# Turns of the second layer's x between the products, two kinds of stores on another queue, and a shared first normalization

## The chip, the cores and the metric

The kernel runs on one core of a Trainium2 chip. The metric is the time of one execution on the device in microseconds; of several runs the median is given. A profiled execution is a run of its own, and the trace is taken from it.

## The reference

Two layers of the same kind are applied to x of shape (32, 32, 64, 256): 32 samples s, 32 places b, 64 channels, 256 positions l. Each layer normalizes x over 32 groups of 8 positions, convolves it along l with weights that are different for every b and l, and adds the result to x. The weights and the bias come from two small networks on z.

```python
h = relu(layernorm(z @ W1 + b1, g1, be1))            # (b, l, 128)
w = (h @ W2 + b2).reshape(B, L, CI, CO, K)           # weights of their own for every b and l
hb = relu(layernorm(z @ Wb1 + bb1, gb1, beb1))
bias = (hb @ Wb2 + bb2).transpose(0, 2, 1)
xp = pad(x, one zero at either end of l)
x_uf = stack([xp[..., i:i + L] for i in range(3)], axis=-1)
conv = einsum('sbilk,bliok->sbol', x_uf, w) + bias[None]
x = x + conv(groupnorm(x))                           # layer 0, then layer 1 with its own parameters
```

In the document the first and the second layer are called layer 1 and layer 2.

## The kernel before

All is in float32. A unit is four places b and a quarter of l (64 positions); a layer has 32 units, so u runs from 0 to 63, and each unit is done in two halves of the output channels. The steps are numbered v = 2u + h, from 0 to 127. `weights(v, k)` for k from 0 to 11 makes one piece of the convolution's weights on TensorE (`make`, lines 633 and 634, into a PSUM tile `pg`, of which there are three) and moves it with the bias b2 into `wall` (`take`, VectorE in line 645, ScalarE in line 656 for half of the third kind). `products(v)` multiplies the normalized x (`xn`) with `wall` in four quarters (line 687, into PSUM tiles `pc`, of which there are two), and VectorE adds each quarter to the residual in `ring` (line 696).

The order of all instructions on each engine is the order of the program text, written out by hand. Step v runs the twelve pieces of `weights(v)`; `products(v - 1)` stands behind the matmuls of the first piece and ahead of its `take`. Behind piece k stand the functions that `agenda(v)` has put into `todo[k]`: statistics, stores, loads (all on the queue of SP), normalization (`normalize`, line 619, on GpSimd) and the addition of the bias to the residual two steps ahead (`add_bias`, line 577, on GpSimd).

The normalized x of a unit stands with samples and places across the free axis in `xn`, which has room for two units. In layer 1 x is loaded in that order from the host's array. In layer 2 x is what layer 1 has stored (`x1`): `parts_of_half` (line 172) loads half of a unit's places with four DMAs into `raw` (first halves) or `land` (second halves), and `turn_half` (line 190) turns it on VectorE in two transpositions of 33 blocks of 32 x 32, one for each pair of places, behind pieces 2 and 3 of a step. `next_half` then normalizes it in place.

Before step 1 stands `first_phase`. Its twenty rounds i compute the hidden layers of both networks in eight batches (`Batch`; tiles of staging lie in `xn` and `raw`, which have no x yet), store the hidden activations (hd, line 317) and the bias (bd, line 339) in DRAM, take statistics of the first groups (line 464), and make the weights of step 0 from round 7 on. At its end `Merge` and `Table` lay out mean and deviation (`tab`), and `starting` normalizes unit 0 in four cuts on VectorE; the cuts 2 and 3 stand between the quarters of `products(0)`.

Of the kernel before, what the change touches and what calls it, by code (L numbers as in the profile page):

```python
# [43 lines left out]
def conv_layers(  # L44
# [142 lines left out]
    def turn_half(u, k, t, buf):  # L187

        src = at(buf[:, t * CH * MT : t * CH * MT + 1], [[1, MH], [MT, CH]])
        nc.vector.transpose(xn[:, u % 2, k * NT // 2 + t], src)  # L190
# [36 lines left out]

    class Batch:


        def __init__(self, nets, zt, zp, zs, j):
            self.j, self.zt, self.zp, self.zs = j, zt, zp, zs
            self.w = nets[j * NR // (UL // 2)]
            flat = xn.rearrange("p n t j s -> p (n t j s)")
            o = 0

            def take(n):
                nonlocal o
                o += n
                return flat[:, o - n : o]  # L240

            ht = [take(2 * BLK) for _ in range(2)]
            self.bs = [take(BLK // 2).rearrange("p (t a m) -> p t a m", t=NT, a=2) for _ in range(4)]
            self.var = take(2 * NR * NR)
            o = flat.shape[1] // 2
            self.ht = [[take(2 * BLK) for _ in range(2)], ht]
            self.q = take(BLK)
            self.zq = take(2 * BLK).rearrange("p (n f) -> p n f", n=2)

# [37 lines left out]
        def turn(self):  # L287
            p = ps_g.tile([P, 2, BLK], FP, tag="pg", name="pz")
            for net in range(2):
                for b in range(NR):  # L290
                    nc.tensor.transpose(
                        p[:, net, b * P : (b + 1) * P],
                        self.zs[:, net, b * NR : (b + 1) * NR].rearrange("p r a -> p (r a)"),
                        ident,
                    )
            nc.scalar.copy(self.zq, p)

        def hidden(self, net):
# [8 lines left out]
            for k in range(2):  # L307
# [7 lines left out]
                if net:  # L315
                    continue
                nc.sync.dma_start(out=hd[self.j * NR // 2 + k], in_=self.ht[0][k])

        def bias(self, i):
            n = 2 * M  # L320
            p = ps_c.tile([P, n], FP, tag="pc", name="pb")
            for b in range(2):
# [16 lines left out]
            nc.sync.dma_start(  # L339
                out=bd[i].rearrange("t b o l -> (b o) t l"), in_=bs.rearrange("p t a m -> p t (a m)")  # L340
# [105 lines left out]
    def first_phase(first_weights, first_bias, add_bias, starting):  # L446
# [22 lines left out]
        with tc.tile_pool(name="stage", bufs=1) as stage:  # L469
# [36 lines left out]
            for i in range(needed + 2):  # L506
# [20 lines left out]
                if i == needed + 1:  # L527
                    merge.mean()
                    merge.root()
                    table.expand(nc.vector)  # L530
                stats(i, range(2))
# [21 lines left out]
                if i == needed + 1:  # L553
                    table.lay(table.spread(), [nc.vector.tensor_copy, nc.scalar.copy])
                    starting(0)
                    starting(1)
# [5 lines left out]
    with tc.manual_schedule():  # L562
# [113 lines left out]
        def products(v, between=None):  # L676
            u, h = divmod(v, NH)
            n = u // UL
            y = residual(v)
            eb = EB // 2  # L680
            for q in range(NB):
                pc = ps_c.tile([P, EB, CH], FP, tag="pc", name="pc")
                for p in range(q * eb, (q + 1) * eb + 1):
                    n0, n1 = max(2 * p - 2, q * EB), min(2 * p + 2, (q + 1) * EB)
                    a = p * F + (n0 - 2 * p) * CH
                    for t in range(NT):
# [7 lines left out]
                        )  # L694
                part = y[:, :, :, q * eb : (q + 1) * eb]
                nc.vector.tensor_tensor(part, pc.rearrange("p (m a) o -> p a o m", a=2), part, ALU.add)  # L696
                if between:
                    between(q)
# [70 lines left out]
        def starting():  # L769
# [5 lines left out]
            def cut(q):  # L775
                if q < NB:
                    for k in range(2):
                        normalize(0, k, bufs[k], nc.vector, cuts[q], cuts[q + 1])
# [19 lines left out]
        def agenda(v):  # L798
# [9 lines left out]
            if UL <= half[0] < U:  # L808
                for t in range(NT // 2):
                    todo[2 + t].append(lambda t=t: turn_half(*half, t, place_half(*half)))  # L810
            todo[3 if half[0] >= UL else 2].append(lambda: next_half(*half))
# [8 lines left out]
            elif x < U:  # L820
                for i, part in zip((1, 1, 4, 4), parts_of_half(x, k, place_half(x, k))):
# [141 lines left out]
```

## Time and profile before

| | us |
|---|---|
| median of 3 runs | 3988.72 |
| lowest and highest run | 3983.26, 3991.18 |
| the profiled execution | 3984.39 |
| its span in the trace | 3982.6 |

The page of the profile gives for each engine the time in which it was busy, as a share of the span. PE is TensorE's matmuls, PEld its loading of weights, which overlaps them; DVE is VectorE, ACT ScalarE, POOL GpSimd, SP the engine that issues the DMAs. L645 is line 645 of the kernel. A row of the waits gives who waited for whom, the sum in microseconds, how often, and the longest. A row of the timeline gives start, duration, engine, line, operation, the tiles as out<-in, the shapes, and in brackets the idle time of the engine ahead of it with what ended it; xN at the end joins N such instructions in a row.

### The profile page before, as it was taken

The page shows a single profiled execution, that of the slowest core. Times are in us where ns is not written, and L with a number is a line of the kernel's source. Part 1 is how long each engine was busy: PE and PEld are TensorE (multiplying, and loading weights), DVE is VectorE, ACT ScalarE, POOL GpSimd, SP SyncE. Part 2 cuts the span into 40 slices and gives each one's busy share as a digit, 9 for nine tenths or more (in the row PEclk, how much of TensorE's full clock was granted, in tenths as well). Part 3 has the DMA queues.
Part 4 walks back from the last instruction along what each step waited for, and adds up shares of the span by engine and source line. Part 5 has one row for each costly group of instructions (what it writes and reads, how often), then busy time and mean ns, then how long its engine had stood idle before and what let it go on. Part 6 is the DMA issues. An engine that isn't in the chain of part 4 may idle for free.

```text
span 3982.6 us, 185486 instructions
## 1 busy us (share of the span) xinstructions
PE 3792.1 (95%) x86548; PEld 3663.0 (92%) x86548; DVE 2813.2 (71%) x3086; ACT 1278.0 (32%) x4399; POOL 1864.3 (47%) x655
## 2 busy tenths in 40 slices
PE   6799999999999999999999999999999999999999
PEld 3699999999999999999989999999999999999998
DVE  5777777777777776767676766666666667666765
ACT  3332333323333333333332332232233223322232
POOL 2255455454554545445444455455445444544452
PEclk8899999999999999999999999999999999999999
DMA  8765655656555554545565555565555555555552
GB/s 288 266 204 173 208 167 196 189 176 207 165 197 189 192 161 135 174 134 172 162 174 143 156 138 133 154 154 134 137 152 150 133 142 155 142 132 146 155 136 87
DMA packets 136756, 657.76 MB, mean 165 GB/s; under 512 B 38312, under 2 KB 45872, under 8 KB 70192
## 3 DMA queue, kind: packets, MB, share of 16 engines
q1 hardware_dynamic: 135984, 645.89, 55.2%
q8 instruction: 677, 11.09, 1.2%
q14 instruction: 95, 0.78, 0.1%
HBM read 496.91 MB, written 148.90 MB: 162 GB/s over the span
## 4 chain that ended last, share of the span: by engine, by line
PE 81%; DVE 8%; issue 7%; DMA 2%; ACT 0%; DVEq 0%; POOL 0%; SPq 0%; ACTq 0%; POOLq 0%
PE pg L633 51%; PE pc L687 24%; PE pg L634 5%; DVE wall L645 5%; DVE xn L190 3%; DMA out_dram<-ring 1%; DMA hd<-xn 0%; ACT xn L308 0%; DMA land<-in_xg_dram 0%; PE spread L422 0%; PE ph L306 0%; DVE ring L696 0%; PE over L377 0%; PE pb L324 0%; DMA hT<-hd 0%
## 5 line engine op out<-in xcount | busy, mean ns | idle before, releaser
L633 PE MATMUL pg<-hT,w2t 128*64 128x128 f32 x24576 | 2754.7, 274 | 118.7 <-DVE wall L645 100.1
L633 PEld LDWEIGHTS pg<-hT,w2t 128*64 128x64 f32 x24576 | 2686.6, 137 | 166.0 <-DVE wall L645 115.8
L634 PE MATMUL pg<-hT,w2t 128*64 128x128 f32 x24576 | 2754.7, 274 | 3.2 <-issue 2.9
L634 PEld LDWEIGHTS pg<-hT,w2t 128*64 128x64 f32 x24576 | 2687.1, 137 | 2.5 <-issue 2.3
L645 DVE TENSOR_TENSOR wall<-pg,b 128x1024 f32<-128x1024 f32 (+1 forms) x1540 | 1866.9, 1218 | 525.7 <-PE pg L634 520.3
L656 ACT ACTIVATE wall<-pg,b 64x128 f32<-64x128 f32 x4064 | 1152.6, 468 | 2586.6 <-DVE wall L645 2586.5
L687 PE MATMUL pc<-wall,xn 128*32 128x128 f32 (+1 forms) x36864 | 946.8, 262 | 24.8 <-issue 18.9
L687 PEld LDWEIGHTS pc<-wall,xn 128*32 128x32 f32 x36864 | 909.8, 110 | 63.3 <-issue 58.0
L577 POOL TENSOR_TENSOR ring<-ring,bt 128x2048 f32<-128x2048 f32 x127 | 580.4, 4570 | 772.0 <-DMA bt<-bd 431.4
L619 POOL TENSOR_TENSOR xn<-xn,tab 128x2112 f32<-128x2112 f32 x190 | 891.1, 4690 | 15.0
L696 DVE TENSOR_TENSOR ring<-pc,ring 128x512 f32<-128x512 f32 x512 | 354.1, 692 | 582.5 <-PE pc L687 504.4
L613 POOL COPY xn<-edge 64x64 f32<-64x64 f32 x96 | 22.3, 232 | 930.9 <-DVE xn L190 589.8
L619 POOL TENSOR_TENSOR xn<-raw,tab 128x2112 f32<-128x2112 f32 x54 | 254.0, 4703 | 172.0 <-PE pc L687 124.1
L347 DVE BATCH_NORM_STATS2 parts<-ring 128x6 f32<-128x256 f32 x512 | 192.2, 417 | 6.5
L190 DVE STREAM_TRANSPOSE xn<-land 128x1056 f32<-128x1056 f32 x64 | 132.6, 2071 | 0.0
L190 DVE STREAM_TRANSPOSE xn<-raw 128x1056 f32<-128x1056 f32 x64 | 132.2, 2066 | 0.0
L739 DVE BATCH_NORM_STATS2 first_parts<-land 128x6 f32<-128x512 f32 x168 | 114.2, 680 | 5.5 <-DMA land<-in_xg_dram 5.4
L439 POOL COPY tab<-spot 64x1024 f32<-64x1024 f32 x28 | 29.0, 1036 | 72.1 <-ACT spot L426 71.2
L282 POOL TENSOR_TENSOR raw<-w2t,xn 128x256 f32<-128x256 f32 x16 | 10.1, 629 | 107.4 <-DVE xn L277 107.4
L464 DVE BATCH_NORM_STATS2 first_parts<-ring 128x6 f32<-128x512 f32 x72 | 44.6, 679 | 10.5 <-DMA ring<-in_xg_dram 10.4
L306 PE MATMUL ph<-xn,wc 17*128 17x512 f32 x128 | 34.6, 745 | 16.4 <-ACT xn L308 6.5
L306 PEld LDWEIGHTS ph<-xn,wc 17*128 17x128 f32 x128 | 9.9, 206 | 35.0 <-ACT xn L308 13.5
(88 smaller groups left out, 413.0 us busy)
## 6 DMA issues: line engine op xcount, KB each, us to landing
bt<-bd SPq DMA_DIRECT2D x508, 256.0 KB, 11.9
ring<-in_xs_dram SPq DMA_DIRECT2D x64, 1024.0 KB, 9.5
x<-ring SPq DMA_DIRECT2D x64, 1024.0 KB, 5.0
ring<-x SPq DMA_DIRECT2D x64, 1024.0 KB, 10.2
out_dram<-ring SPq DMA_DIRECT2D x64, 1024.0 KB, 5.1
raw<-in_xp_dram SPq DMA_DIRECT2D x55, 1056.0 KB, 12.3
land<-in_xg_dram SPq DMA_DIRECT2D x46, 1024.0 KB, 8.4
raw<-x SPq DMA_DIRECT2D x128, 256.0 KB, 8.6
```

What stands on the lines that cost most here:

```text
L190: nc.vector.transpose(xn[:, u % 2, k * NT // 2 + t], src)
L347: nc.vector.bn_stats(out, y[:, :, :, g * e : (g + 1) * e])
L464: nc.vector.bn_stats(first_parts[:, g, bg], slots[order[i]][:, k])
L577: nc.gpsimd.tensor_tensor(y, y, bts.pop(v).rearrange("p o (a m) -> p o a m", a=2), ALU.add)
L619: eng.tensor_tensor(o, i, tab[:, x, None, j0:j1].to_broadcast(list(o.shape)), op)
L633: nc.tensor.matmul(pg[0:C, k, :], w[:, k0 * C : (k0 + 1) * C], h0, start=True, stop=True)
L634: nc.tensor.matmul(pg[C:P, k, :], w[:, k1 * C : (k1 + 1) * C], h1, start=True, stop=True)
L645: nc.vector.tensor_tensor(place(rows, a), pg[rows].rearrange("p o (t m) -> p t m o", t=NT), b2[n][rows, kind, None, None, o0 : o0 + OG].to ...
L656: nc.scalar.activation(place(rows, a)[:, :, :, k], pg[rows, k].rearrange("p (t m) -> p t m", t=NT), AF.Identity, bias=b2[n][rows, kind, o0 ...
L687: nc.tensor.matmul(pc[t * S : (t + 1) * S, n0 - q * EB : n1 - q * EB, :], xn[:, u % 2, t, p, :], wall[:, t, a : a + (n1 - n0) * CH], start ...
L696: nc.vector.tensor_tensor(part, pc.rearrange("p (m a) o -> p a o m", a=2), part, ALU.add)
L739: nc.vector.bn_stats(first_parts[:, g, bg], lands[i % LAND])
```

## The change

- In layer 2 each transposition of a half is cut in two (17 and 16 columns), and the four instructions of a half are put into `products(u, h)` for the half h of the next unit: two ahead of the eviction of the first quarter, one behind that, one behind the second. `next_half` for that half stands behind piece 0 of the next step, and the loads of a half (`parts_of_half`) stand one step later than before.
- The stores of hd and bd are issued from ScalarE's queue. Each is owed until the next call of `pay`, which stands behind a later instruction of ScalarE.
- `q` of a batch lies in `raw`, and `bs`, the bias on its way to bd, lies in the second half of `xn`, no more in the first.
- The laying out of the first table and the first two cuts of `starting` stand ahead of the last round's statistics; of each cut the first pair of places is normalized on VectorE and the second on GpSimd.

```diff
-    def turn_half(u, k, t, buf):
-        src = at(buf[:, t * CH * MT : t * CH * MT + 1], [[1, MH], [MT, CH]])
-        nc.vector.transpose(xn[:, u % 2, k * NT // 2 + t], src)
+    def turns_of_half(u, k, buf):
+        def turn(t, j0, j1):
+            i = t * CH * MT + j0
+            src = at(buf[:, i : i + 1], [[1, j1 - j0], [MT, CH]])
+            nc.vector.transpose(xn[:, u % 2, k * NT // 2 + t, j0:j1], src)
+        cuts = (0, MH // 2 + 1, MH)
+        return [lambda t=t, c=c: turn(t, *c) for t in range(NT // 2) for c in zip(cuts, cuts[1:])]
...
+    owed = []
+    def pay(*stores):
+        for f in owed:
+            f()
+        owed[:] = stores
...
+            self.q = raw[:, 2 * BLK : 3 * BLK]
...
-            self.bs = [take(BLK // 2).rearrange("p (t a m) -> p t a m", t=NT, a=2) for _ in range(4)]
             self.var = take(2 * NR * NR)
...
-            self.q = take(BLK)
             self.zq = take(2 * BLK).rearrange("p (n f) -> p n f", n=2)
+            self.bs = [take(BLK // 2).rearrange("p (t a m) -> p t a m", t=NT, a=2) for _ in range(4)]
...
             nc.scalar.copy(self.zq, p)
+            pay()
...
                 if net:
-                    continue
-                nc.sync.dma_start(out=hd[self.j * NR // 2 + k], in_=self.ht[0][k])
+                    pay()
+                else:
+                    pay(lambda k=k: nc.scalar.dma_start(out=hd[self.j * NR // 2 + k], in_=self.ht[0][k]))
...
-            nc.sync.dma_start(
-                out=bd[i].rearrange("t b o l -> (b o) t l"), in_=bs.rearrange("p t a m -> p t (a m)")
+            pay(
+                lambda: nc.scalar.dma_start(
+                    out=bd[i].rearrange("t b o l -> (b o) t l"), in_=bs.rearrange("p t a m -> p t (a m)")
+                )
             )
...
+                if i == needed + 1:
+                    table.lay(table.spread(), [nc.vector.tensor_copy, nc.scalar.copy])
+                    starting(0)
+                    starting(1)
+                    pay()
                 stats(i, range(2))
...
-                if i == needed + 1:
-                    table.lay(table.spread(), [nc.vector.tensor_copy, nc.scalar.copy])
-                    starting(0)
-                    starting(1)
...
+            turns = turns_of_half(u + 1, h, place_half(u + 1, h)) if UL <= u + 1 < U else []
...
+                if turns and q == 0:
+                    turns.pop(0)()
+                    turns.pop(0)()
                 part = y[:, :, :, q * eb : (q + 1) * eb]
                 nc.vector.tensor_tensor(part, pc.rearrange("p (m a) o -> p a o m", a=2), part, ALU.add)
+                if turns:
+                    turns.pop(0)()
...
-                    for k in range(2):
-                        normalize(0, k, bufs[k], nc.vector, cuts[q], cuts[q + 1])
+                    for k, eng in enumerate((nc.vector, nc.gpsimd)):
+                        normalize(0, k, bufs[k], eng, cuts[q], cuts[q + 1])
...
-            if UL <= half[0] < U:
-                for t in range(NT // 2):
-                    todo[2 + t].append(lambda t=t: turn_half(*half, t, place_half(*half)))
-            todo[3 if half[0] >= UL else 2].append(lambda: next_half(*half))
+            if half[0] < UL:
+                todo[2].append(lambda: next_half(*half))
+            if u + 1 >= UL:
+                todo[0].insert(0, lambda: next_half(u + 1, h))
...
-            elif x < U:
-                for i, part in zip((1, 1, 4, 4), parts_of_half(x, k, place_half(x, k))):
+            if UL <= half[0] < U:
+                for i, part in zip((1, 1, 4, 4), parts_of_half(*half, place_half(*half))):
```

## Rows read from the trace of the kernel before

**Rows 1.** The page: span, and each engine's busy time, share and instructions.
```profile
span 3982.6 us, 185486 instructions
...
PE 3792.1 (95%) x86548; PEld 3663.0 (92%) x86548; DVE 2813.2 (71%) x3086; ACT 1278.0 (32%) x4399; POOL 1864.3 (47%) x655
```
**Rows 2.** Waits of TensorE's weight loads in 1000:2000 (layer 1): us, times, longest.
```profile
PEld pg L633 <- DVE wall L645: 1.8, 1, 1.8
```
**Rows 3.** The same in 2100:3900 (layer 2).
```profile
PEld pg L633 <- DVE wall L645: 102.9, 59, 1.8
```
**Rows 4.** Timeline of VectorE, one step of layer 2.
```profile
2479.01 1.22 DVE L645 TENSOR_TENSOR wall<-pg,b 128x1024 f32<-128x1024 f32 x1 [0.52 <-PE pg L634]
2482.72 0.69 DVE L696 TENSOR_TENSOR ring<-pc,ring 128x512 f32<-128x512 f32 x1 [2.49 <-PE pc L687]
2484.41 0.69 DVE L696 TENSOR_TENSOR ring<-pc,ring 128x512 f32<-128x512 f32 x1 [1.00 <-PE pc L687]
...
2492.68 2.07 DVE L190 STREAM_TRANSPOSE xn<-land 128x1056 f32<-128x1056 f32 x1
...
2495.70 2.07 DVE L190 STREAM_TRANSPOSE xn<-land 128x1056 f32<-128x1056 f32 x1
...
2512.69 0.69 DVE L696 TENSOR_TENSOR ring<-pc,ring 128x512 f32<-128x512 f32 x1 [2.49 <-PE pc L687]
```
**Rows 5.** Timeline of VectorE, first evictions of two steps at the end.
```profile
3914.70 0.69 DVE L696 TENSOR_TENSOR ring<-pc,ring 128x512 f32<-128x512 f32 x1 [2.49 <-PE pc L687]
...
3942.96 0.69 DVE L696 TENSOR_TENSOR ring<-pc,ring 128x512 f32<-128x512 f32 x1 [2.49 <-PE pc L687]
```
**Rows 6.** Lines 190 and 390 on VectorE: count, ns minimum/median/maximum, first and last.
```profile
L190 DVE STREAM_TRANSPOSE xn<-raw x64: 1999/2070/2107, 1972.1 to 3867.7; 128x1056 f32<-128x1056 f32 x64
...
L390 DVE TENSOR_TENSOR apart<-over,moments x9: 144/157/163, 153.0 to 2047.6; 128x8 f32<-128x8 f32 x5, 128x9 f32<-128x9 f32 x1, 128x2 f32<-128x2 f32 x1, 128x6 f32<-128x6 f32 x1
```
**Rows 7.** Timelines of VectorE and GpSimd, a turn beside the laying of a table.
```profile
2462.68 2.03 DVE L190 STREAM_TRANSPOSE xn<-raw 128x1056 f32<-128x1056 f32 x1
...
2462.44 1.03 POOL L439 COPY tab<-spot 64x1024 f32<-64x1024 f32 x1 [9.96 <-ACT spot L426]
```
**Rows 8.** Loads into `raw`: SP's timeline, and time to landing in 2100:3900.
```profile
2493.25 1.16 SPq L172 DMA_DIRECT2D raw<-x  x2
...
DMA to landing us min/median/max: 5.4/8.6/12.8
```
**Rows 9.** Timeline of GpSimd in the step of rows 4.
```profile
2498.44 9.46 POOL L619 TENSOR_TENSOR xn<-xn,tab 128x2112 f32<-128x2112 f32 x2
2507.90 4.57 POOL L577 TENSOR_TENSOR ring<-ring,bt 128x2048 f32<-128x2048 f32 x1
```
**Rows 10.** The first products: timelines of TensorE and VectorE, and the chain of work.
```profile
165.70 0.45 PE L633 MATMUL pg<-hT,w2t 128*64 128x128 f32 x1 [8.35 <-issue]
...
169.38 2.52 PE pc L687 x72
...
166.54 0.76 DVE L619 TENSOR_TENSOR xn<-land,tab 128x576 f32<-128x576 f32 x1 [3.82 <-DMA bd<-xn]
...
182.36 0.69 DVE L696 TENSOR_TENSOR ring<-pc,ring 128x512 f32<-128x512 f32 x1 [0.66 <-PE pc L687]
```
**Rows 11.** Timeline of VectorE, first statistics of a piece in step 1.
```profile
200.66 0.69 DVE L739 BATCH_NORM_STATS2 first_parts<-land 128x6 f32<-128x512 f32 x1 [5.43 <-DMA land<-in_xg_dram]
```
**Rows 12.** First phase: ScalarE, TensorE, line 339, and busy time by engine in 60:70.
```profile
51.14 4.63 ACT L308 ACTIVATE xn<-ph,vec 128x1024 f32<-128x1024 f32 x4 [3.31 <-DMA hd<-xn]
...
68.98 0.45 PE L633 MATMUL pg<-hT,w2t 128*64 128x128 f32 x1 [5.01 <-DMA hT<-hd]
...
L339 SPq DMA_DIRECT2D bd<-xn x32: 360/456/2676, 36.5 to 162.8; - x32
...
60.00:70.00 10.00, 4.46 (x30) 2.14 (x28) 2.85 (x7) 6.03 (x9) 6.89 (x6) 0.74 1.05 368
```

## The prediction

> **What bounds the kernel now.** I read the page first: TensorE is busy 95% of the span and VectorE 71%, so a microsecond counts only where TensorE stands still [rows 1]. Next I read who TensorE's weight loads waited for, in layer 1 and in layer 2 apart. In 1000 us of layer 1 they waited 1.8 us for VectorE, once; in 1800 us of layer 2 they waited 102.9 us for line 645, 59 times and at most 1.8 us, which is once in every step [rows 2, 3]. Line 645 (`take`) empties the PSUM tiles of the weight products. Why it is late only in layer 2 is seen in VectorE's timeline of one step [rows 4]: behind the third and the fourth `take` stands a transposition of line 190 of 2.07 us (2492.68 and 2495.70), 4.1 us in all. A `take` without them has 0.52 us of idle time ahead of its 1.22, so TensorE makes a tile every 1.74 us, and it has three PSUM tiles to run ahead with. The step from the first eviction of line 696 to the next one takes 2512.69 - 2482.72 = 29.97 us. A step of layer 2 without transpositions stands at the very end: 3942.96 - 3914.70 = 28.26 us [rows 5]. So the transpositions cost 1.71 us per step where they stand.
>
> **Part 1, the turns move into the products.** There are 64 transpositions from `raw` and as many from `land`, two to a step, so 64 steps [rows 6]. The change cuts each in two (17 and 16 of 33 columns) and issues two halves ahead of the first eviction of line 696, one behind the first and one behind the second. In these places VectorE waits for TensorE anyway: 2.49 us ahead of the first eviction and 1.00 us ahead of the second [rows 4]. The price of a half: 2.07 us / 33 = 0.063 us a column, so 1.07 and 1.00 us, and a cut adds what a VectorE instruction costs beside its columns. The trace of before has no half turn; the bounds are nothing, and the 0.16 us that a VectorE instruction on 8 elements takes as a whole [rows 6]. Two halves take 2.07 to 2.23 us in a gap of 2.49: hidden. The third, 1.07 to 1.23 us in a gap of 1.00, makes the second eviction 0.07 to 0.23 us late, the fourth adds at most 0.1. The products have two PSUM tiles: the third quarter needs the first one's tile, which is free from 2482.72 + 0.69 = 2483.41, while the second quarter is finished at 2484.41 [rows 4]. So an eviction may be 0.9 to 1.0 us late before TensorE notices. The `take`s are then left alone on VectorE, 1.22 us of every 1.74, as in the step of 28.26 us.
> Sum of part 1: 64 x 1.71 = **-109.4 us**. The waits give the same from another side: 102.9 / 59 x 64 = 111.6 us [rows 3]. I take the smaller.
>
> What moves with it: the loads of a half (line 172, four DMAs on SP's queue) come one step later, and so have less time. The last two are issued at 2493.25 to 2494.41, and such loads land 8.6 us after their issue, 12.8 at most [rows 8]: at 2503, at worst 2507.2. The first half turn now stands right behind the last `take` of the step, which ended 2479.01 + 1.22 = 2480.23 in the step shown; one step of 28.26 us later that is 2508.5. It holds by 1.3 us in the worst case and 5.5 in the middle one, and 0.26 us of gap plus 0.9 of PSUM slack stand behind that. What waits behind a late load on VectorE would be the four evictions, and behind them TensorE. The normalization on GpSimd (two instructions of 9.46 us together [rows 9] and the edges, some 10 us) now starts in the middle of the products and not behind the second turn, which is earlier in the step; its result is needed one step later, at the next unit's or half's products, so it has some 12 us to spare, and some 7 us where the tables are laid first. The addition of the bias (4.57 us) follows it on GpSimd and is for the products a step further on. The loads of edges on SP's queue go ahead of the store, half a microsecond each, with nothing to wait for. I cost these at nothing.
>
> **Part 2, stores on ScalarE's queue, other staging.** 16 stores of hd and 32 of bd leave SP's queue; on SP the issue of one of bd took 0.46 us in the median, 0.36 to 2.68 [rows 12]. No trace shows a store issued from ScalarE. I take SP's median for all. Each is put off until ScalarE's next piece of work is done, so it waits for nothing; behind it on ScalarE stand the activations of line 308 and 333, and behind those the weight matmuls. In seven of the batches one store of bd lies between the two activations that free the PSUM tiles for the next matmuls: 7 x 0.46 = +3.2 us. The others fall into ScalarE's idle time. Bounds: all 48 on the path, 48 x 0.46 = +22.1 us, or none.
> What SP's queue gains: one activation waited 3.31 us for a store of hd, and the first weight matmul waited 5.01 us for the load of hd, which stood in SP's queue behind stores [rows 12]. At most 8.3 us are to be had. But in this stretch the DMA engines are full (share 1.05 at 368 GB/s), so a store that goes early delays a load; only what falls behind the load of hd helps, about 1 MB (two stores of bd of 128 KB and most of two of hd of 512 KB, by the size of their tiles): 1 MB / 368 GB/s = -2.7 us. I take -2.7, bounds 0 and -8.3.
>
> **Part 3, the first normalization.** One of its instructions on VectorE waited 3.82 us for a store of bd, because the staging lay in the place it writes [rows 10]. That goes, and GpSimd takes half. But it isn't what TensorE waits for: the first products start at 169.38 behind weight products that start at 165.70, after 8.35 us of idle time that the trace calls issue [rows 10]. These are the first that read the second half of W2, a load of 3 MB, the one operand that is not there. So the start stays. During the first products VectorE has two normalizing instructions (0.76 us for the first cut) per quarter in place of four. A quarter's matmuls take 2.52 us, so the four could end at 169.38 + 10.1 = 179.5 and their last eviction is at 182.36 now [rows 10]: at most -2.9 us. Soon after, VectorE stands 5.43 us for a piece of x in `land` [rows 11], whose load stands in SP's queue behind a load into `raw`, which waits for the last reading of `raw` by VectorE, some 1.2 us earlier now. I take **-1.2 us**.
> Parts 2 and 3: 3.2 - 2.7 - 1.2 = -0.7 us; bounds -11.2 and +22.1.
>
> **Sum.** The profiled run took 3984.4 us (span 3982.6 and 1.8 around it): 3984.4 - 109.4 - 0.7 = 3874.3. The median of the runs is 4.3 us above the profiled run, so the forecast is **3878 us**, between 3878 - 2.2 - 10.5 = 3865 and 3878 + 22.8 = 3901.
>
> **Rivals.**
> 1. The turns are hidden in part. If halves or late loads make the first eviction later than the 0.3 us of gap and 0.9 of slack, TensorE stands in the products. A loss of 0.4 to 1 us in each of 64 steps gives back 26 to 64 us: 3904 to 3942. Against it: the gaps of the rows 4 repeat in the step of rows 5. For it: loads that land at their worst leave 1.3 us.
> 2. VectorE's turns and GpSimd's long instructions exclude each other. Now GpSimd waits until a turn is over; in the changed kernel the first two halves fall under the addition of the bias, which runs from 2507.90 to 2512.47 in the step shown [rows 9]. If a half had to wait for its end, the first eviction would come at 2512.5 + 2.1 = 2514.6 and not at 2482.72 + 28.26 = 2510.98: 3.6 - 0.9 = 2.7 us in each step, +173 us against -110: **4052 us**. It would decide for slower from a wait of 1.71 + 0.9 = 2.6 us on. Against it: eight turns ran while GpSimd copied tables, and took no longer, 2.03 us beside copies that took 1.03 as ever [rows 7]. The Trainium skill, page "SBUF — State Buffer", section "Who interferes with whom", says that VectorE and GpSimd share one port pair under an exclusive lock, and that a VectorE instruction with two SBUF inputs blocks against a GpSimd instruction that reads SBUF, while one with at most one input outside the two-port modes does not. By that the turns, with one input, are safe, as rows 7 have it, and the normalization shared in part 3, with two inputs on either engine, runs one after the other; no run here shows that. With the start at 169.38 there is time for that too.
> 3. TensorE does not take the time: the stall turns up again as "issue" or in another wait, and the step stays near 30 us. 3988 us. Steps of 28.26 us with the same work on TensorE speak against it [rows 5].
>
> **Chances.** Forecast 0.80, rival 1 0.12, rival 2 0.04, rival 3 0.04. The range takes in the forecast's own bounds and the mild end of rival 1: 3860 to 3905. A measurement of this kernel can tell 0.2%, 8 us, from no change. Faster: forecast and rival 1, 0.92; same: rival 3, 0.04; slower: rival 2, 0.04.
>
> **What would show it.** In the timeline of a layer 2 step the halves must end ahead of the first eviction and the step be 28.3 us; the waits of weight loads for line 645 must be near nothing in layer 2, and those of line 687 must not grow. Turns longer than 1.1 us under the addition of the bias would show rival 2; a VectorE wait for `raw<-x` or `land<-x` rival 1. In the first 200 us the weight matmuls should start a few us before 68.98 and the first products still follow the load of W2. The forecast is wrong if the first evictions of layer 2 are late by more than 0.9 us.

## The result, and the profile after

The changed kernel took 3919.71 us (median of four runs, 3918.21 to 3923.92) against 3989.92 us for the kernel before on the same chip: a ratio of 0.9829, 95% interval 0.9812 to 0.9846. That is 70 us faster. The forecast was 3878 us, 110 us faster, and 3919.71 lies above the end of its range, 3905. So the direction was right and the size of the main term was not what reached the clock.

The page of the changed kernel (its profiled run took 3918.21 us). Line numbers have moved: `take` is now line 662 on VectorE and 673 on ScalarE, the weight matmuls 650 and 651, the products' matmuls 705, their eviction 717, the turns 192, the normalization 636, the addition of the bias 594 and its loads 587.
```profile
span 3916.4 us, 185576 instructions
...
PE 3791.8 (97%) x86548; PEld 3667.1 (94%) x86548; DVE 2855.3 (73%) x3205; ACT 1276.2 (33%) x4399; POOL 1878.0 (48%) x664
...
q8 instruction: 676, 11.08, 1.2%
```
Against [rows 1], TensorE has the same number of instructions and 0.3 us less of busy time; the 66.2 us that the span lost are all idle time. The last row comes into play below.

VectorE's timeline in layer 2 of the changed kernel (start, duration, instruction, idle time before it and its end). The evictions of other quarters and all `take`s are left out:
```profile
2591.22 0.69 DVE L717 TENSOR_TENSOR ring<-pc,ring 128x512 f32<-128x512 f32 x1 [0.41 <-issue]
...
2616.90 2.18 DVE L192 STREAM_TRANSPOSE xn<-land 128x544 f32<-128x544 f32 x2
2619.49 0.69 DVE L717 TENSOR_TENSOR ring<-pc,ring 128x512 f32<-128x512 f32 x1 [0.41 <-PE pc L705]
2620.10 1.14 DVE L192 STREAM_TRANSPOSE xn<-land 128x544 f32<-128x544 f32 x1
2621.56 0.69 DVE L717 TENSOR_TENSOR ring<-pc,ring 128x512 f32<-128x512 f32 x1 [0.33 <-PE pc L705]
2622.17 1.10 DVE L192 STREAM_TRANSPOSE xn<-land 128x512 f32<-128x512 f32 x1
...
2650.40 0.69 DVE L717 TENSOR_TENSOR ring<-pc,ring 128x512 f32<-128x512 f32 x1 [2.08 <-issue]
...
2680.17 0.69 DVE L717 TENSOR_TENSOR ring<-pc,ring 128x512 f32<-128x512 f32 x1 [0.42 <-issue]
...
2708.43 0.69 DVE L717 TENSOR_TENSOR ring<-pc,ring 128x512 f32<-128x512 f32 x1 [0.39 <-issue]
```
The two halves of 2616.90 are done 0.41 us ahead of the first eviction, and the other two fit between the evictions, as planned. From 2591.22 to 2619.49 the step takes 28.27 us, and so does the one that ends at 2708.43 (28.26): the forecast step to the hundredth. But between them stand steps of 30.91 and 29.77 us. In layer 2 the first eviction of step 64 is at 2062.88 and that of step 125 at 3847.65, so 61 steps take 29.26 us in the mean; only 21 of them stay within 0.2 us of the shortest. In the kernel before, the same 61 run from 2060.21 to 3914.70, 30.40 in the mean, and 37 of them stay within 0.2 us of 29.96. Something lengthens steps in both kernels, and in the changed one it does so more often: by 1.0 us in the mean against 0.44.

What TensorE's weight loads waited for in 2100:3900 (total us, times, longest), first the kernel before, below the row shown in [rows 3], then the changed one:
```profile
PEld pc L687 <- issue: 23.0, 85, 0.8
PEld pg L633 <- issue: 6.0, 8, 1.5
PEld pg L634 <- issue: 0.8, 2, 0.6
```
```profile
PEld pc L705 <- issue: 27.6, 102, 0.9
PEld pg L651 <- issue: 17.2, 18, 1.5
PEld pg L650 <- issue: 15.6, 21, 1.6
PEld pg L650 <- ACT wall L673: 0.6, 1, 0.6
```
The 102.9 us of [rows 3] are gone; of waits for a `take` only the last row, 0.6 us, is left. In their place "issue", a wait for nothing that the profile names, has gone from 29.8 to 60.4 us, above all in the weight matmuls (6.8 to 32.8). The same 61 steps should have saved 61 x 1.71 = 104.3 us and saved 1854.5 - 1784.8 = 69.7: 34.6 are missing, and the growth of these waits makes 30.6 of them.

**One such wait, from near.** In the step that begins at 2619.49, TensorE's weight loads break off, and the profile names no engine and no load that they wait for (timeline of weight loads):
```profile
2644.90 0.14 PEld L651 LDWEIGHTS pg<-hT,w2t 128*64 128x64 f32 x1
2646.64 0.13 PEld L650 LDWEIGHTS pg<-hT,w2t 128*64 128x64 f32 x1 [1.60 <-issue]
```
The DMA queues (packets, MB, share of 16 engines) in 2629:2643.5, and then in 2643.5:2645.5:
```profile
q1 hardware_dynamic: 740, 3.51, 100.8%
q8 instruction: 1, 0.02, 0.5%
```
```profile
q1 hardware_dynamic: 107, 0.20, 47.8%
q8 instruction: 1, 0.02, 4.1%
```
Queue 8 moves 11.08 MB in 676 packets of 16 KB over the run. TensorE has 86548 matmuls and as many weight loads, 173096 instructions, or 256 for each packet: this queue brings TensorE's instructions. In the 14.5 us in which the step's data (store, x, residual, bias) fill the DMA engines it got a single packet through. The next one starts as the data thin out; its 1.3 us (4.1% of 16 engines x 2 us) end at about 2645.2, and 1.4 us later TensorE goes on. Of the 47 waits of weight loads over 0.4 us in 2100:3830, 45 end 1.2 to 1.7 us after the end of such a packet; of all weight loads in this window only a tenth start at such a distance from one.

How fast TensorE uses them is read from a table by stretches (behind the length: busy time and instructions of TensorE's matmuls, its weight loads, VectorE, ScalarE and GpSimd; then granted clock, DMA share, GB/s). The stretches are the products, the data transfers in two parts, and the wait.
```profile
2619.50:2625.50 6.00, 5.53 (x208) 5.00 (x199) 4.13 (x5) 0.00 (x0) 2.87 (x4) 1.00 0.01 3
2629.00:2636.00 7.00, 7.00 (x134) 7.00 (x130) 4.89 (x4) 4.03 (x16) 4.21 (x1) 1.00 1.00 284
2636.00:2643.00 7.00, 7.00 (x133) 7.00 (x130) 4.89 (x4) 2.78 (x11) 0.00 (x0) 1.00 1.04 210
2645.00:2650.00 5.00, 3.64 (x101) 3.23 (x100) 3.21 (x3) 0.19 (x1) 4.00 (x1) 1.00 0.03 8
```
In the products TensorE uses 407 instructions in 6 us, 256 in 3.8 us; in the weight matmuls 264 in 7 us, 256 in 6.8 us. While the data run, packets came some 9 us apart (2625.8, 2634.9, 2643.8), so each falls 2.2 us behind, until what TensorE holds is used up. From the end of the packet of 2625.8, at 2626.8, to the break at 2645.0 it used some 676 instructions and got 256, so it held some 420 when the transfers began. Over the 61 steps the longest pause between two such packets is 9.3 us in the median step. The kernel before has the same transfers, but it reached this point 1.71 us later, having stood still for VectorE meanwhile. That is theory F of the experiments. It was formed from these rows, so it had to be tried.

### The profile page after: what moved, and what is told of

It is laid out like the page before. It is cut to its first block, busy times and chain, and to the rows that moved or that the text cites. A ratio compares the mean times of both kernels' runs of the same rounds, so it can differ in the third digit from the quotient of the medians.

```text
span 3916.4 us, 185576 instructions
## 1 busy us (share of the span) xinstructions
PE 3791.8 (97%) x86548; PEld 3667.1 (94%) x86548; DVE 2855.3 (73%) x3205; ACT 1276.2 (33%) x4399; POOL 1878.0 (48%) x664
## 3 DMA queue, kind: packets, MB, share of 16 engines
q8 instruction: 676, 11.08, 1.2%
## 4 chain that ended last, share of the span: by engine, by line
PE 93%; issue 1%; DMA 1%; POOL 0%; DVE 0%; ACT 0%; SPq 0%; POOLq 0%; ACTq 0%
PE pg L650 62%; PE pc L705 24%; PE pg L651 7%; POOL xn L636 0%; DMA land<-in_xg_dram 0%; PE over L393 0%; PE spread L438 0%; PE pe L614 0%; DMA raw<-in_xp_dram 0%; DVE wall L662 0%; DVE xn L636 0%; DVE ring L717 0%; ACT tab L455 0%; DVE first_parts L762 0%; DVE parts L363 0%
## 5 line engine op out<-in xcount | busy, mean ns | idle before, releaser
L636 POOL TENSOR_TENSOR xn<-xn,tab 128x2112 f32<-128x2112 f32 (+1 forms) x194 | 897.7, 4627 | 37.9 <-PE pc L705 21.9
L192 DVE STREAM_TRANSPOSE xn<-land 128x544 f32<-128x544 f32 (+1 forms) x128 | 140.5, 1118 | 0.0
L192 DVE STREAM_TRANSPOSE xn<-raw 128x544 f32<-128x544 f32 (+1 forms) x128 | 140.3, 1116 | 0.0
L636 POOL TENSOR_TENSOR xn<-land,tab 128x2112 f32<-128x2112 f32 (+2 forms) x12 | 43.9, 3655 | 22.1 <-ACT tab L457 22.1
## 6 DMA issues: line engine op xcount, KB each, us to landing
raw<-in_xp_dram SPq DMA_DIRECT2D x55, 1056.0 KB, 12.2
```

The costliest lines, as they stand in the source:

```text
L192: nc.vector.transpose(xn[:, u % 2, k * NT // 2 + t, j0:j1], src)
L636: eng.tensor_tensor(o, i, tab[:, x, None, j0:j1].to_broadcast(list(o.shape)), op)
```

## The experiments

Theory F says that TensorE's instructions come late because data occupy the DMA engines. Its rivals: G, the moved turns or loads delay TensorE themselves; H, the move gave its 109 us and the rest of the change lost 40; J, raised by a later run, that the bias was late for GpSimd. An edit is against the changed kernel where nothing else is said. Each ratio is to the kernel before, run beside it on the same chip. Differences to the changed kernel are of medians from different chips; worked out from the ratios they come out up to some 6 us otherwise.

**Turns alone.**
To the kernel before (the loads of x one step later belong to it):
```diff
-            if UL <= half[0] < U:
-                for t in range(NT // 2):
-                    todo[2 + t].append(lambda t=t: turn_half(*half, t, place_half(*half)))
...
+            turns = turns_of_half(u + 1, h, place_half(u + 1, h)) if UL <= u + 1 < U else []
...
```


> The kernel before with the turns of the second layer moved between the products, and nothing else of the change. Three explanations of why the change gained 70 us and not 110. Theory F (late instructions): with VectorE's 1.71 us out of the way, TensorE stands in the same stretch of many steps because its next block of instructions has not come, so the move alone gives about 64 x 1.1 = 70 us: 3915 to 3920 us. Theory G (work in the way): the half turns themselves or the earlier loads delay TensorE: the same 3915 to 3920 us, told apart by the run without turns. Theory H (the rest of the change loses it): the move alone gives the forecast 109 us, 3880 us, and stores and first normalization cost 40.

3914.01 us; ratio to the kernel before 0.9821 (0.9806 to 0.9835). The waits named issue came to 66.4 us in 2100:3900 (29.4 + 24.2 + 12.8). H falls: the move alone gains what the whole change gains.

**All but the turns.**
To the changed kernel (the loads of x with it, as before):
```diff
-            turns = turns_of_half(u + 1, h, place_half(u + 1, h)) if UL <= u + 1 < U else []
...
+            if UL <= half[0] < U:
+                for t in range(NT // 2):
+                    todo[2 + t].append(lambda t=t: turn_half(*half, t, place_half(*half)))
...
```


> The whole change but for the turns, which stay ahead of the first eviction as in the kernel before: stores from ScalarE's queue, staging moved, first normalization shared with GpSimd. By F and G: within 5 us of the kernel before, 3985 to 3995 us. By H: 25 to 40 us slower, 4015 to 4030 us.

3985.01 us; ratio 0.9999 (0.9989 to 1.0008). Stores, staging and first normalization together are worth nothing that can be measured; the forecast had -0.7 us for them.

**No turns at all.**
```diff
-            turns = turns_of_half(u + 1, h, place_half(u + 1, h)) if UL <= u + 1 < U else []
+            turns = []
```


> The changed kernel with the transpositions of the second layer left out altogether (the products of that layer then use stale halves; loads, normalizations and all else stay). F: the turns cost nothing where they now stand, so the time stays within 5 us of the changed kernel, 3915 to 3923 us, and TensorE's waits for nothing seen in the second layer stay near 59 us. G: without them the forecast time comes out, about 3880 us.

3915.80 us, 0.9835 (0.9807 to 0.9862); the changed kernel has 0.9829. Waits of weight loads in 2100:3900:
```profile
PEld pc L705 <- issue: 29.1, 100, 1.6
PEld pg L650 <- issue: 15.1, 19, 1.6
PEld pg L651 <- issue: 14.6, 14, 2.3
```
58.8 us of the same waits without a single turn. Where they now stand the turns are free, and G falls for them.

**No loads of the bias in layer 2.**
```diff
+            if u > UL:
+                bts[v] = last[0]
+                return
-            bts[v] = bp.tile(...)
+            bts[v] = last[0] = bp.tile(...)
```


> The changed kernel with the loads of the bias in the second layer left out (the last one loaded in the first layer is added each time): 1 MB less of transfers behind each step's last eviction, while every instruction of TensorE, VectorE's turns and the additions stay. F: the block of instructions comes sooner, TensorE's waits for nothing seen in the second layer fall from 59 us to under 30, the step goes from 29.3 to 28.5 us and the time to about 3880 us (3870 to 3895). G: the turns and loads of x stand where they stood, 3915 to 3923 us.

3872.90 us, 0.9718 (0.9703 to 0.9732). The waits:
```profile
PEld pc L709 <- issue: 20.2, 81, 1.6
PEld pg L654 <- issue: 1.8, 5, 0.4
```
60.4 us have become 22.0, and 32.8 of the weight matmuls 1.8, with no instruction of TensorE changed. F predicted this, but J would as well. The turns and the loads of x stand where they stood, so G falls for the loads too.

**One more transfer.**
```diff
...
+            if UL <= u < U - 1:
+                loads[6].append(lambda: nc.sync.dma_start(out=spare[v % 2], in_=x1[0][h]))
```


> The changed kernel with one more transfer in each step of the second layer: 1 MB copied within DRAM, issued by SyncE behind the loads of the bias, read by nobody. The bias lands as before, so does everything else. Theory F (TensorE's instructions come late because data transfers occupy the DMA engines until about 23 us after a step's first eviction): the busy stretch grows by at least 4 us, TensorE's waits for nothing seen rise from 59 us to 90 to 160, time 3945 to 4020 us. Theory J (leaving out the bias helped because the addition of the bias on GpSimd no longer waits for its load): nothing that a result waits for is changed, 3915 to 3925 us.

3979.54 us, 0.9984 (0.9972 to 0.9996): 60 us lost to a transfer that nothing waits for. The waits:
```profile
PEld pc L706 <- issue: 62.8, 143, 2.0
PEld pg L651 <- issue: 27.3, 25, 3.1
PEld pg L652 <- issue: 22.5, 17, 3.3
```
112.6 us, 52 more than in the changed kernel, and 89 of the 94 waits over 0.4 us end 1.2 to 1.7 us after an instruction packet. F stands and J falls, since the bias was as early as ever: 12.1 us from issue to landing in the median, 12.2 in the changed kernel.

**Bias loads from ScalarE's queue.**
```diff
...
-                loads[6] = [lambda: load_bias(v + 1), ...]
+                loads[6] = [lambda: load_bias(v + 1, eng=nc.scalar if u >= UL else nc.sync), ...]
```


> The changed kernel, but the bias loads of the second layer are issued from ScalarE's queue in its order of work (at the seventh group of weights of a step) and not by SyncE behind the other loads. The same bytes in each step. F: the bytes still run without a break through the same stretch or a little later, so no more than part of the 59 us is saved or some is added: 3895 to 3930 us. J: the bias lands later, the addition on GpSimd waits longer, slower: 3930 to 3960 us.

4057.69 us, 1.0187 (1.0172 to 1.0202), far from either number.
```profile
PEld pg L650 <- DVE wall L662: 178.7, 114, 1.6
```
TensorE now waits for the emptying of PSUM, which ScalarE shares and into which its four issues of a step fall; and as it stands still there, the issue waits drop to 15.8 us (12.7 + 2.4 + 0.7), as they had been lower in the kernel before. That fits F, but the run tells nothing on the place of the transfers. Why four issues of 0.3 to 0.45 us cost 2.2 us per step wasn't settled.

**Loads one step earlier.**
```diff
+            if NH * UL + 1 <= v < NH * U - 2:
+                todo[10].append(lambda: load_residual(v + 2))
+                todo[10].append(lambda: load_bias(v + 2))
 (and no load_residual(v + 1), load_bias(v + 1) in these steps)
```


> The changed kernel, but in the second layer the residual and the bias of a step are loaded one step earlier, behind the addition of the bias and so during the products, where the DMA engines are idle now (the first 6 us and the last 4 us of a step counted from its first eviction). The same bytes, in two stretches of some 8 us in place of one of 16. F: each stretch is over before TensorE has used up what instructions it holds; its waits for nothing seen fall from 59 us to under 35, the step from 29.3 to 28.5 us, time 3860 to 3890 us. If the bytes in all are what counts and not the length of a stretch: 3915 to 3925 us.

3874.00 us, 0.9724 (0.9709 to 0.9738): with all of the work done, 46 us faster than the changed kernel and 111 us faster than the kernel before. A step of it, from first eviction at 2635.83 (columns as in the table by stretches above):
```profile
2641.80:2653.00 11.20, 11.20 (x210) 11.20 (x208) 8.49 (x8) 4.56 (x16) 11.12 (x3) 1.00 0.95 255
2653.00:2654.30 1.30, 1.30 (x30) 1.30 (x27) 0.79 (x1) 0.00 (x0) 0.72 (x1) 1.00 0.61 239
2654.30:2659.50 5.20, 5.20 (x100) 5.20 (x98) 3.62 (x4) 3.45 (x13) 0.00 (x0) 1.00 0.90 205
```
The transfers did not move into the products, as expected: the residual runs on behind x, and the bias waits until GpSimd has added the former one. What there is, is a thinner 1.3 us at 17 us after the first eviction and a shorter second part. It is enough: the issue waits fall to 25.2 us (20.3 + 4.5 + 0.4). Instruction packets come at 2647.3, 2653.7 and 2659.8, and the longest pause between two is 7.7 us in the median step, where it was 9.3. The same bytes, so bytes in all are not what counts.

**All four halves ahead of the first eviction.**
```diff
-                if turns and q == 0:
-                    turns.pop(0)()
-                    turns.pop(0)()
+                while turns:
+                    turns.pop(0)()
...
```


> The changed kernel with all four half turns of a step ahead of its first eviction (in the change two stand ahead of it and one behind each of the next two). 4 x 1.1 = 4.4 us against a gap of 2.49 us and 0.9 us of slack in PSUM: TensorE waits about 1 us for the first eviction in each of 63 steps. By the working of the prediction 20 to 65 us slower than the changed kernel: 3940 to 3985 us. If VectorE's place in the products is as free as the run without turns says, the same 3920 us.

3942.52 us, 0.9899 (0.9884 to 0.9913): 23 us slower than the changed kernel. VectorE's timeline, and the wait of weight loads that this makes:
```profile
2477.36 4.20 DVE L192 STREAM_TRANSPOSE xn<-raw 128x544 f32<-128x544 f32 x4
2481.49 1.23 DVE L716 TENSOR_TENSOR ring<-pc,ring 128x512 f32<-128x512 f32 x2
```
```profile
PEld pc L705 <- DVE ring L716: 34.3, 50, 0.8
```
The last `take` ended at 2477.44, so the first eviction would stand at 2477.44 + 2.49 = 2479.93 and comes 1.56 us late; TensorE waits 0.69 us (34.3 / 50). The slack in PSUM is 0.87 us where the prediction worked out 0.9 to 1.0. Of the 34.3 us, 12 come back in the issue waits (60.4 to 47.8): a stall ahead of a late block of instructions pays for part of itself.

**Early loads in the kernel before.** The same edit as in the early loads, in the kernel before:
```diff
+            if NH * UL + 1 <= v < NH * U - 2:
+                todo[10].append(lambda: load_residual(v + 2))
+                todo[10].append(lambda: load_bias(v + 2))
...
```

> The kernel before, its turns where they were, with nothing but the early loads of the second layer: residual and bias of a step issued one step earlier, behind the addition of the bias. F: in this kernel the 1.71 us in which TensorE waits for VectorE already gave its instructions the time to come, so the break in the transfers saves only what is left of the 30 us of waits for nothing seen: 3965 to 3985 us, and the waits for VectorE's copies stay near 103 us. With the early loads in both kernels the moved turns are then worth the forecast 64 x 1.71 = 109 us: 3874 + 109 = 3983. If the early loads gave their 45 us for a reason of their own: 3935 to 3945 us.

4102.98 us, 1.0295 (1.0279 to 1.0312): a miss. The waits of weight loads for issue in the products, and SyncE's issue of the bias in one step:
```profile
PEld pc L687 <- issue: 65.4, 83, 3.7
```
```profile
2733.00 2.34 SPq L570 DMA_DIRECT2D bt<-bd  x4
```
The first eviction of that step is at 2733.26. In this kernel the normalization starts behind the second turn, so GpSimd's addition is over later, and the bias is loaded in the products, where TensorE uses 256 instructions in 3.8 us. The issue waits come to 110.7 us (65.4, and 22.7 + 22.6 in the weight matmuls), 81 more than before. The edit did another thing in this kernel than in the changed one, so the run doesn't price the turns; the 118 us lost are named, though. Over the 61 steps used above the loss is 115.3 us (first evictions at 2057.52 and 4027.34, 1969.8 against 1854.5), and the issue waits grew by 90 (30.2 to 120.2). The rest is TensorE's clock: after some of the long waits it runs on at half speed (table by stretches; the sixth column behind the length is the granted clock):
```profile
2285.90:2289.00 3.10, 0.01 (x1) 0.00 (x0) 0.00 (x0) 0.00 (x0) 0.00 (x0) 1.00 0.04 8
2289.10:2292.50 3.40, 3.40 (x41) 3.21 (x42) 1.82 (x2) 0.00 (x0) 0.00 (x0) 0.50 0.30 120
```
These 61 steps have 14 such stretches at 0.50, the lower of the two levels, each beside a wait for issue of 1.8 to 3.5 us. They last 51 us, so 26 us at full speed are lost; the same steps of the kernel before have none.

**Early loads in both layers.**
Against the run with early loads in layer 2:
```diff
-            if NH * UL + 1 <= v < NH * U - 2:
+            if 5 <= v < NH * U - 2:
```


> The changed kernel with the early loads from the sixth step on, so in the first layer too, where TensorE's waits for nothing seen came to 19 us in 900. F: at most some 30 us are there to be saved in the 58 steps of the first layer, so 3855 to 3874 us. If the first layer's waits have another source: 3870 to 3880 us, as with the early loads in the second layer alone.

3973.27 us, 0.9972 (0.9962 to 0.9981): a miss of the same kind. In layer 1 the bias is issued at 1533.34, and the third quarter's eviction of those products waits:
```profile
1546.73 0.69 DVE L717 TENSOR_TENSOR ring<-pc,ring 128x512 f32<-128x512 f32 x1 [4.29 <-PE pc L705]
```
In 1000:1900 the weight loads of the products waited 43.6 us for issue, against 12.3 in the changed kernel. The granted clock fell here too, to 0.50 from 1544.4 to 1547.8 in the step shown; in steps 8 to 63 that costs 31 us of full speed, against 3 with the early loads in layer 2 alone. Layer 2 ran as with the early loads there alone (28.58 us a step in both).

**No loads of the bias, in the kernel before.** The edit of the run without loads of the bias, in the kernel before:
```diff
+            if u > UL:
+                bts[v] = last[0]
+                return
...
```

> The kernel before with the loads of the bias in the second layer left out, in the same way as in the changed kernel (the last one of the first layer is added each time), and no other edit. F: the stretch of transfers is over early, but TensorE's instructions had time to come in the 1.71 us for which it waits for VectorE, so little is saved: of the 30 us of waits for nothing seen about 10 go, 3970 to 3985 us, and the wait for VectorE's copies stays 59 times 1.74 us. Against the changed kernel with the same loads left out (3873) the moved turns are then worth 97 to 112 us, the size that the prediction gave them. If the bias loads cost every kernel the same 45 us: 3935 to 3945 us, and the turns are worth 70 us in either pair.

3973.36 us, 0.9965 (0.9951 to 0.9978).
```profile
PEld pg L638 <- DVE wall L650: 104.8, 60, 1.9
PEld pc L692 <- issue: 19.2, 78, 1.0
```
Leaving out 1 MB per step is worth 14 us here and 47 us in the changed kernel: the stall for VectorE had covered most of the late instructions. With these loads out of both kernels the moved turns are worth (0.9965 - 0.9718) x 3987 = 98 us, with the two intervals 90 to 106. The two profiled spans differ by 3980.6 - 3867.2 = 113.4, but they were the slowest of five runs and the fastest of four. Steps can be compared without that: the 61 steps used above take 3912.62 - 2067.75 = 1844.9 us in this run and 3798.26 - 2059.71 = 1738.6 in the changed kernel without these loads, 106.3 less. The forecast's 61 x 1.71 is 104.3.

**Bias ahead of the residual.**
Against the run with early loads in layer 2:
```diff
-                todo[10].append(lambda: load_residual(v + 2))
                 todo[10].append(lambda: load_bias(v + 2))
+                todo[10].append(lambda: load_residual(v + 2))
```


> The changed kernel with the early loads in the second layer, bias ahead of the residual. SyncE holds the residual back too until GpSimd has added the bias, so the store and the parts of x run in one stretch of some 7 us, and bias and residual in another of 7 to 8 us, with a break of about 4 us between them where there was one of 1 to 2. F: as with the early loads or a little better, 3855 to 3876 us, waits for nothing seen at or under 23 us. If the residual then comes too late for the addition on GpSimd: 3880 to 3920 us.

3916.95 us, 0.9826 (0.9812 to 0.9839): a miss, all that the early loads had gained is gone. The break is there, but the second part of the transfers now ends just ahead of the products, whose first eviction is at 2678.85 (table by stretches, then the wait):
```profile
2668.00:2676.50 8.50, 8.50 (x168) 8.33 (x168) 6.40 (x6) 4.53 (x16) 0.00 (x0) 1.00 0.94 255
2676.50:2684.00 7.50, 7.10 (x274) 6.68 (x269) 5.31 (x7) 0.00 (x0) 1.80 (x3) 1.00 0.03 7
```
```profile
PEld pc L705 <- issue: 54.4, 152, 1.6
```
The waits have left the weight matmuls (3.4 us in all) for the products (20.3 with the early loads, 54.4 here); 58 of the 61 over 0.4 us end 1.2 to 1.7 us after an instruction packet. So a longer break isn't better by itself: what counts is what TensorE uses while and right after the data run. That reading came after the run; it agrees with the two misses before it and was not tried apart from them.

## Why the prediction was right in direction and too high in gain

**The step that failed** is the one that set the length of the new step. "A step of layer 2 without transpositions stands at the very end" [rows 5], 28.26 us, was taken as the length of every step without them; measured were 29.26 us in the mean of 61 steps. That step differed in a second respect: nothing of x is loaded for a step that no longer comes. The DMA part of the page for 3915:3943 of the kernel before, and for 2483:2512.5 (the step of [rows 4]):
```profile
DMA packets 487, 3.24 MB, mean 116 GB/s; under 512 B 96, under 2 KB 96, under 8 KB 96
```
```profile
DMA packets 966, 4.35 MB, mean 147 GB/s; under 512 B 192, under 2 KB 320, under 8 KB 576
```
1.1 MB less, which is what the run without loads of the bias took away. That step was the floor and not the mean: the shortest step of the changed kernel takes 28.25 us too.

**The price of the turns was right.** Undisturbed steps went from 29.96 to 28.25 us, the 1.71 of the forecast. Where the bias isn't loaded and few instructions come late, 61 steps give 106.3 us, 1.74 each, and the medians of the whole runs 98 (90 to 106) against the 109.4 for 64 steps. In the changed kernel 70 arrive, since 31 to 35 us come back as waits for instructions.

**Rival 3** ("the stall turns up again as issue") was the right mechanism and got 0.04, with a price of everything or nothing. What spoke for it was in the view of [rows 3]: 29.8 us of issue waits, which the prediction didn't weigh. A third of the gain, given back in some of the steps, was in no rival by this mechanism. Among what would show it, "those of line 687 must not grow" looked at the wrong line: they grew by 4.6 us, those of the weight matmuls by 26.

**Rivals 1 and 2.** The measured 3920 us lies among the 3904 to 3942 of rival 1, but that is chance: the turns left the first eviction in its place, and with no turn at all the time stays at 3915.80. The forecast's own sign of being wrong, first evictions late by more than 0.9 us, did not come. The halves of 17 columns took 1.15 us in the mean and those of 16 columns 1.08, within the bounds, and no turn waited for its load. Beside GpSimd they were not slowed: 1.15 us for the 68 halves of 17 columns that ran beside a TENSOR_TENSOR of GpSimd, 1.15 for the 27 that ran beside none. GpSimd's addition of the bias over the two halves of 2616.90 kept its time too (timeline of GpSimd):
```profile
2615.57 4.58 POOL L594 TENSOR_TENSOR ring<-ring,bt 128x2048 f32<-128x2048 f32 x1 [11.03 <-DMA edge<-xe]
```
4.58 us as in [rows 9]. The run without turns and that with four halves ahead confirm the placing: 0 and +23 us.

**Parts 2 and 3** were -0.7 in the forecast and 0 within 4 us in the run. Their single terms were not right, though. Issues on ScalarE's queue took 0.34 us for hd and 0.38 for bd in the median, not 0.46. The 5.01 us wait for the load of hd [rows 12] is down to 0.68, yet the first weight matmul came at 71.1 and not "a few us before 68.98", behind other waits. The first products still start where W2 lets them, 169.72 against 169.38 [rows 10], as forecast, and the first eviction at 171.80 against 172.0. Their last eviction came at 180.25 against 182.36, 2.1 us earlier where the forecast allowed 2.9 and took 1.2. The 2.9 was no true bound, though: the 2.52 us for a quarter [rows 10] was read in 169.38:171.90, where the granted clock was 0.77, and at full clock two evictions stand 1.69 us apart [rows 4]. In the first cut the sharing saved VectorE nothing: its two instructions, beside GpSimd's, took 2.00 and 1.77 us, in place of four of 0.76. The piece of x that cost 5.43 us [rows 11] cost 9.35 in the changed kernel's profile and 3.08 in that of the turns alone: these first steps vary by more than the term.

## What to carry to other kernels

Where TensorE waits for nothing that the profile names, look at the DMA table for a queue called instruction and at where the data transfers lie in the step: an engine that runs out of instructions looks like that. A stall taken away doesn't return whole if it covered another; read the other waits of the same view as a second price, and compare with a step that differs in one respect alone. In this kernel long, unbroken transfers did least harm where TensorE uses few instructions per microsecond, and did harm in the stretch where it uses many and, by one run, right before it.

## What the runs showed of the hardware that was not expected

- TensorE's instructions arrive as 16 KB packets of 256 over the DMA engines that move the data. Beside transfers at full share (1.00 to 1.04) they came some 9 us apart in the step shown, beside none as fast as they were used (3.8 us). The Trainium skill, page "Runtime: NRT & Kernel Launch", section "Instruction fetch mechanics", describes blocks of this size fetched ahead by the engine's own DMA queue, and calls the cost mostly hidden. The size agrees with 676 packets for 173096 instructions; that it is hidden doesn't, in this kernel: 60.4 us of layer 2 are named issue, and 22.0 with 1 MB less of data per step.
- A long wait for instructions can cost more than its length. In the run with early loads in the kernel before, 14 stretches at a granted clock of 0.50, 3.4 us each and once 6.8, stand beside waits of 1.8 to 3.5 us; other waits as long have none beside them.
- In the shared first normalization, VectorE's instruction was slowed by GpSimd's. The first of these rows is VectorE's beside GpSimd's below it, the second, of the same shape, is after GpSimd had finished:
```profile
172.41 1.58 DVE L636 TENSOR_TENSOR xn<-raw,tab 128x512 f32<-128x512 f32 x1
...
175.89 0.68 DVE L636 TENSOR_TENSOR xn<-raw,tab 128x512 f32<-128x512 f32 x1
```
```profile
172.16 1.28 POOL L636 TENSOR_TENSOR xn<-xn,tab 128x512 f32<-128x512 f32 x1
```
  1.58 against 0.68 us. The rule of the Trainium skill that rival 2 cites (page "SBUF — State Buffer", section "Who interferes with whom": two inputs in SBUF block, at most one does not) agrees with both sides: these have two inputs, and the turns, with one, kept their time.
